# Products for the row maxima over 64 queries of two heads, in an attention and FFN layer on one core

## The chip, the cores and the metric

One core of a Trainium2 chip runs the whole layer in one launch. The metric is the device time of an execution in microseconds; three runs of the kernel before took 827.39, 828.68 and 829.8 us, and their median, 828.68 us, is the time before.

## What is computed

The input `x` is 4 sequences of 512 tokens with 1024 features, in float32. With LN for a layer norm without weights, the layer is:

```python
q = LN(x) @ Wq                        # 32 heads of 32
k, v = split(LN(x) @ Wkv)             # one head of keys and values, shared by the 32
scores = q·k / sqrt(32) + slope[h] * (key_pos - query_pos)     # ALiBi
attn = softmax(scores where key_pos <= query_pos)              # causal
x = x + (attn @ v) @ Wo
w = (six-bit codes unpacked from qweight - zero_point) * scale
x = x + (LN(x) @ w.T + bias)
```

## The kernel before

Products run on TensorE (PE) in `fp32r`; where one such product is not exact enough, both operands are cut in a high and a low part and two or three products are summed (`split` makes the parts: ScalarE copies the high part, VectorE subtracts to get the low one).

**Attention** is done in 32 steps: 4 sequences (`b`) by 8 groups (`g`) of 4 heads (`GH`). The step `i = b * 8 + g` has three parts, and at any time the parts of several steps are under way:

- `queries` computes the 128 rows (4 heads by 32) of q for 512 tokens in 24 products (line 682), splits them into `qh` and `ql`, writes both to the DRAM buffer `q_d` and reads them back three times (high, low, high) into one *query stack* `qs`: rows 0 to 95 are q, 28 more rows (`qr_d`, prepared once for each group) hold the ALiBi slopes and the block-wise causal mask, and two last rows will hold the row maxima. There are three buffers for such stacks. A step so moves 256 KB five times through `q_d`, in runs of 2 KB, and 224 KB from `qr_d`. The moves are issued on SP's queue by the helper at line 420.
- `maxima` needs the largest score of each query and head. It multiplies a block of queries (as weights, 128 columns of the stack) with the keys that it may see (moving). For token tile `t` of 128 queries and head `h` the keys up to `(t + 1) * 128` are taken (line 739): 16 products, four each with 512, 384, 256 and 128 columns. They fill 11 PSUM banks in turn (`S_BANKS`), of which two are there. VectorE adds the triangle `mask` and takes the maximum of each row in one instruction for each product (line 752), into one column of `mx`; the bank is free again after it. One transpose (line 768) turns `mx` into 16 rows of 128, ScalarE and VectorE cut them in two parts `mt`, and two DMAs put them into the last rows of the stack.
- `attention` multiplies the keys (as weights) with the stack: the result `st` (line 820) is the score less the maximum, transposed (keys in partitions). ScalarE takes the exponential into `p`; GpSimd clears what lies above the diagonal, for each of the four key tiles one selection over 4 heads by 128 queries (line 839); `pav` (line 849) multiplies with the values, four heads side by side in the array; GpSimd adds up the `p` of the four tiles (line 861), and `den` (line 878) sums over keys. `a` is copied to DRAM; the denominators are inverted at a sequence's end (`invert`).

After that come 16 token tiles with the output projection `po` (line 1048), the second layer norm and the FFN product `pf` (line 1168). They use nothing of what is changed here.

**Order.** Each operation is written with a wished-for time (`at`), a cost in ns and what it reads and writes. A planner (`Work`) plays the engines forward and backward with these costs and puts out one fixed order for each engine; DMAs count as 450 ns of SP each and then a rate of 280 bytes per ns and 2 us to land, whatever the length of their runs. At run time each engine works its list strictly in that order, and waits where an operand is not there yet; also an operation that could run has to wait behind one that can't. A changed cost or width anywhere can move operations elsewhere.

The lines that say how a step's products are put into banks:

```python
S_BANKS = [((t, h),) for t in (3, 2) for h in range(GH)]
S_BANKS += [tuple((1, h) for h in (2 * i, 2 * i + 1)) for i in range(2)]
S_BANKS += [tuple((0, h) for h in range(GH))]
```

Of the kernel before, what the change touches and what calls it, by code (L numbers as in the profile page):

```python
# [41 lines left out]
P = 128  # L43
NH = 32
HD = 32
GH = 4
S = 512
# [25 lines left out]
def bias_rows():  # L73

    k = np.arange(S)
    block = k // KB
    kr = np.zeros((N_BIAS + 2, S), np.float32)
    kr[0:2] = k - block * KB - KB // 2  # L80
    for r in range(NB):
        kr[2 + r] = kr[2 + NB + r] = block == r
    kr[N_BIAS:] = -1.0
    slopes = alibi_slopes(NH)
    sh, sl = split12(slopes)
    qr = np.zeros((NH, N_BIAS, S), np.float32)
    qr[:, 0] = sh[:, None]
    qr[:, 1] = sl[:, None]
    r = np.arange(NB)
    mid = r[:, None] * KB + KB // 2 - k[None, :]  # L90
    v = slopes[:, None, None] * mid[None]
    v = np.where((r[:, None] > block[None, :])[None], MASKED, v)
    qr[:, 2 : 2 + NB], lo = split12(v)
    qr[:, 2 + NB :] = np.where(v == MASKED, 0.0, lo)
    qr = qr.reshape(NH // GH, GH, N_BIAS, S).transpose(0, 2, 1, 3)
    return kr, np.ascontiguousarray(qr)
# [245 lines left out]
def layer_kernel(  # L342
# [30 lines left out]
    for name, bufs in (  # L373
        ("const", 1), ("w", 2 * NG), ("xc", KC + 2), ("x", 4), ("qs", 3), ("q1", 1), ("p0", 2),
        ("pj", 1), ("stg", 3), ("kv", 2), ("small", 4), ("mt", 2),
    ):
        pool(name, bufs)
# [41 lines left out]
    def move(dst, src):  # L419
        return nc.sync.dma_start(out=dst.bitcast(F32), in_=src.bitcast(F32))  # L420


    qr_d = tc.dram_tile([NG, N_BIAS, GH, S], F32R, name="qr_d")
    at_d = tc.dram_tile([NG, P, B * S], F32, name="at_d")
    q_d = tc.dram_tile([4, 2, P, S], F32R, name="q_d")
# [16 lines left out]
    nc.gpsimd.affine_select(  # L442
        out=mask(),
        in_=mask(),
        pattern=[[-1, S]],
        compare_op=ALU.is_ge,
        fill=MASKED,
        base=S - P,
        channel_multiplier=1,
    )  # L450
# [14 lines left out]
    def prep_rows(at, g):  # L465
        dma(
            at, 229e3, lambda: nc.gpsimd.dma_start(out=qr_d[g], in_=q_rows[g]), [qr_i[g]], [],
            eng="POOL",
        )
# [205 lines left out]
    def queries(at, i):  # L675
        b, g = divmod(i, NG)
        pq = new("ps_q", "q", [P, S], F32, f"pq_{i}")
        hi, lo = wq[g]
        for c in range(KC):
            def three(c=c):  # L680
                for n, (w, s) in enumerate(((hi, 0), (lo, 0), (hi, 1))):
                    nc.tensor.matmul(  # L682
                        pq(), w()[:, c, :], xc[b, c]()[:, s, :],
                        start=(c == 0 and n == 0), stop=(c == KC - 1 and n == 2),
                    )
            h = c // (KC // 2)
            pe(at + 1.3 * c, [S] * 3, three, [pq], [(hi, h), (lo, h), xc[b, c]], more=12.0)
        at += 10.4
        qh = new("q1", "qh", [P, S], F32R, f"qh_{i}")
        ql = new("q1", "ql", [P, S], F32R, f"ql_{i}")  # L690
        split(at, S, qh, ql, pq, qh, ql, pq)

        qs[i] = [(0, GH, new("qs", "qs", [P, GH, S], F32R, f"qs_{i}"))]
        for s, src in enumerate((qh, ql)):
            dma(
                at + 0.6 + 0.7 * s, 262e3,
                lambda s=s, src=src: move(q_d[i % 4, s], src()), [q_i[i % 4][s]], [src],
            )
        for h, n, q in qs[i]:
            dma(  # L700
                at + 1.0, 57e3 * n,
                lambda h=h, n=n, q=q: move(q()[R_BIAS:R_MAX, :, :], qr_d[g, :, h : h + n, :]),
                [(q, "b")], [qr_i[g]],
            )
            for r in range(3):
                dma(
                    at + 3.0 + 0.1 * r, 65e3 * n,
                    lambda r=r, h=h, n=n, q=q: move(
                        q()[ts(r, HD), :, :],
                        q_d[i % 4, r % 2, h * HD : (h + n) * HD].rearrange(  # L710
                            "(h d) q -> d h q", d=HD
                        ),
                    ),
                    [(q, r)], [q_i[i % 4][r % 2]],
                )

    def part(i, h):

        return next((q, h - first) for first, n, q in qs[i] if first <= h < first + n)


    S_BANKS = [((t, h),) for t in (3, 2) for h in range(GH)]
    S_BANKS += [tuple((1, h) for h in (2 * i, 2 * i + 1)) for i in range(2)]
    S_BANKS += [tuple((0, h) for h in range(GH))]
    ROWS = (0, 1, 2, "b")

    def maxima(at, i):
        b = i // NG
        k = kst[b % 2]
        mx = new("small", "mx", [P, GH * NT], F32, f"mx_{i}")  # L730
        for n, bank in enumerate(S_BANKS):
            ps = new("ps_s", "s", [P, S], F32, f"s_{i}_{n}")
            widths = [(t + 1) * P for t, _ in bank]
            places = [sum(widths[:m]) for m in range(len(bank))]

            def products(ps=ps, bank=bank, widths=widths, places=places):
                for (t, h), W, o in zip(bank, widths, places):
                    q, at = part(i, h)
                    nc.tensor.matmul(  # L739
                        ps()[:, o : o + W], q()[0:R_MAX, at, ts(t, P)], k()[0:R_MAX, :W],  # L740
                        start=True, stop=True,
                    )
            pe(
                at + 1.2 * n, widths, products, [ps],
                [(q, r) for q in {part(i, h)[0] for _, h in bank} for r in ROWS] + [k],
                more=sum(45.0 if w == P else 5.0 for w in widths),
            )
            for (t, h), W, o in zip(bank, widths, places):
                junk = new("q1", "junk", [P, S], F32, f"junk_{i}_{t}_{h}")
                dve(  # L750
                    at + 1.2 * n + 0.3, W,
                    lambda ps=ps, junk=junk, t=t, h=h, W=W, o=o: nc.vector.tensor_tensor_reduce(  # L752
                        out=junk()[:, :W],
                        in0=ps()[:, o : o + W],
                        in1=mask()[:, S - W :],
                        scale=1.0,
                        scalar=-3e38,
                        op0=ALU.add,
                        op1=ALU.max,
                        accum_out=mx()[:, h * NT + t : h * NT + t + 1],  # L760
                    ),
                    [(mx, (t, h))], [ps], more=125.0,
                )
        at += 1.2 * len(S_BANKS)
        N = GH * NT
        tr = new("ps_misc", "misc", [P, P], F32, f"trm_{i}")
        pe(
            at, [P], lambda: nc.tensor.transpose(tr()[0:N, :], mx(), ident()), [tr], [mx]
        )
        for s in range(2):  # L770
            m = new("mt", f"mt{s}", [N, P], F32R, f"mt{s}_{i}")
            if s == 0:
                hi = m
                act(at + 0.2, P, lambda: nc.scalar.copy(hi(), tr()[0:N, :]), [hi], [tr])
            else:
                lo = m
                dve(
                    at + 0.4, P,
                    lambda: nc.vector.tensor_tensor(
                        lo(), tr()[0:N, :], hi().bitcast(F32), ALU.subtract  # L780
# [3 lines left out]
            for h, n, q in qs[i]:  # L784
                dma(
                    at + 0.5 + 0.2 * s, 2e3 * n,
                    lambda m=m, s=s, h=h, n=n, q=q: move(
                        q()[R_MAX + s : R_MAX + s + 1, :, :], m()[h * NT : (h + n) * NT, :]
                    ),
                    [(q, f"m{s}")], [m],  # L790
                )
# [6 lines left out]
    def attention(at, i):  # L798
        b, g = divmod(i, NG)
        k = kst[b % 2]  # L800
# [5 lines left out]
        for n, (j, heads) in enumerate(ST_BANKS):  # L806
# [3 lines left out]
            runs = []  # L810
            for first, m, q in qs[i]:
                lo, hi = max(first, heads[0]), min(first + m, heads[-1] + 1)
                if lo < hi:
                    runs.append((
                        q, slice(lo - first, hi - first), slice(lo - heads[0], hi - heads[0])
                    ))

            def products(ps=ps, j=j, runs=runs):
                for q, mine, place in runs:
                    nc.tensor.matmul(  # L820
                        ps()[:, place, :], k()[0:R_ALL, ts(j, P)], q()[0:R_ALL, mine, j * P :],
                        start=True, stop=True,
                    )
            pe(
                at + 1.2 * n, [len(heads) * W / len(runs)] * len(runs), products, [ps],
                [q for q, _, _ in runs] + [k], more=5.0,
            )
# [8 lines left out]
            if done[j] == GH:  # L836
                def select(j=j):
                    d = pr[j]()[:, :, 0:P]
                    nc.gpsimd.affine_select(  # L839
                        out=d, in_=d, pattern=[[0, GH], [1, P]], compare_op=ALU.is_ge,  # L840
# [26 lines left out]
        act(at + 15.4, S, lambda: nc.scalar.copy(a(), pav()), [a], [pav])  # L867
# [16 lines left out]
    def invert(at, b):  # L884
        r = new("stg", "stg", [P, S], F32, f"rec_{b}")
        d = den[b]
        for t in range(NT):
            work.op(
                "DVE", at + 0.1 * t, 840.0,
                lambda t=t: nc.vector.reciprocal(r()[:, ts(t, P)], d()[:, ts(t, P)]),  # L890
# [410 lines left out]
```

## Time and profile before

| | us |
|---|---|
| median of three runs | 828.68 |
| the profiled execution: its own time | 830.86 |
| its span, from the first to the last instruction | 828.9 |
| busy in the span: TensorE | 802.1 |
| busy: VectorE | 572.4 |
| busy: GpSimd | 515.7 |
| busy: ScalarE | 369.4 |
| mean granted TensorE clock | 0.993 |

The profile is of one execution, by the hardware profiler. A line of its groups names the source line, engine, operation, `out<-in` tiles, partitions by elements, the count, then busy time in us and the mean ns of one, then the idle time of the engine just before such instructions and what ended it. `PEld` is the weight loads of TensorE, which run beside its products; `SPq` is SP's queue, which issues DMAs. The time from the first product to the end of the attention is some 540 us of the span; the token tiles follow until 829 us, the first two of them overlapping the last steps.

### The profile page before, as it was taken

What the parts mean: (1) busy time and instruction counts of PE and PEld (TensorE: products, weight loads), DVE (VectorE), ACT (ScalarE), POOL (GpSimd) and SP (SyncE); (2) the same over time, 40 slices, a digit from 0 to 9 for tenths busy, and PEclk for the clock granted to TensorE, in tenths of its full rate; (3) what the DMA queues carried; (4) which work ended last, traced back from release to release, by engine and by line L of the source; (5) the groups of instructions that cost most, each with busy time, mean ns of one, the idle gap of its engine ahead of it and who ended that gap; (6) DMA issues with size and microseconds to landing.
All of it is one profiled execution on the core that took longest, in us unless ns stands there. A gap on an engine that the chain in (4) does not pass through costs nothing.

```text
span 828.9 us, 13434 instructions
## 1 busy us (share of the span) xinstructions
PE 802.1 (97%) x4480; PEld 595.8 (72%) x4480; DVE 572.4 (69%) x1491; ACT 369.4 (45%) x659; POOL 515.7 (62%) x442
## 2 busy tenths in 40 slices
PE   5989999999999999999999999999999999999997
PEld 5766677776566767666766667667888888888885
DVE  7576876478676469866358656645988867678755
ACT  4336664545665354755365564340142323333320
POOL 4337968285968185876388997778556445554323
PEclk9989999999999999999999999999999999999999
DMA  7997662486742397463457774626975675565321
GB/s 221 245 249 214 186 173 63 123 221 216 207 112 82 91 257 227 116 162 113 153 138 220 200 215 141 232 51 165 254 169 137 138 184 127 137 164 131 102 51 51
DMA packets 131796, 133.39 MB, mean 161 GB/s; under 512 B 42964, under 2 KB 93140, under 8 KB 130704
## 3 DMA queue, kind: packets, MB, share of 16 engines
q1 hardware_dynamic: 130912, 129.01, 57.4%
q0 software_dynamic: 816, 3.53, 1.5%
q8 instruction: 35, 0.57, 0.3%
q14 instruction: 33, 0.27, 0.1%
HBM read 85.58 MB, written 39.85 MB: 151 GB/s over the span
## 4 chain that ended last, share of the span: by engine, by line
PE 87%; DMA 4%; DVE 4%; issue 2%; POOL 1%; ACT 1%; SPq 0%; DVEq 0%; ACTq 0%; POOLq 0%
PE po L1048 21%; PE pq L682 18%; PE pf L1168 13%; PE s L739 9%; PE st L820 9%; PE pav L849 8%; PE den L878 3%; PE pkv L616 2%; PE tr L598 2%; DVE junk L752 2%; POOL p L861 1%; DMA q_d<-ql 1%; DMA qs<-q_d 1%; ACT p L830 1%; DMA qs<-qr_d 1%
## 5 line engine op out<-in xcount | busy, mean ns | idle before, releaser
L752 DVE CUSTOM_DVE_ANT_0 junk<-s,mask 128x256 f32<-128x256 f32 (+3 forms) x512 | 250.4, 489 | 123.2 <-PE s L739 92.1
L861 POOL TENSOR_TENSOR p<-p,p 128x1536 f32<-128x1536 f32 (+2 forms) x96 | 230.4, 2400 | 20.2 <-PE pav L849 18.2
L830 ACT ACTIVATE p<-st 128x512 f32<-128x512 f32 (+1 forms) x352 | 184.0, 560 | 115.1 <-PE st L820 111.7
L682 PE MATMUL pq<-xc,wqh 128*128 128x512 f32 x512 | 195.8, 402 | 1.5 <-DVE ql L415 1.4
L1048 PE MATMUL po<-woh,aT 128*128 128x512 f32 x512 | 165.7, 390 | 0.0
L839 POOL TENSOR_SCALAR_AFFINE_SELECT p<-p 128x512 f32<-128x512 f32 x128 | 81.9, 645 | 104.4 <-ACT p L830 103.7
L739 PE MATMUL s<-kst,qs 124*128 124x256 f32 (+3 forms) x512 | 138.4, 339 | 7.0 <-DVE mx L752 3.3
L820 PE MATMUL st<-qs,kst 126*128 126x512 f32 (+1 forms) x352 | 125.6, 395 | 3.1 <-ACT p L830 2.6
L1168 PE MATMUL pf<-wf,xT 128*128 128x512 f32 x512 | 120.8, 390 | 0.7 <-DVE xT L415 0.7
L739 PEld LDWEIGHTS s<-kst,qs 124*128 124x128 f32 x512 | 89.0, 193 | 44.1 <-DVE mx L752 16.3
L682 PEld LDWEIGHTS pq<-xc,wqh 128*128 128x128 f32 x512 | 97.6, 191 | 21.6 <-DVE ql L415 2.1
L1048 PEld LDWEIGHTS po<-woh,aT 128*128 128x128 f32 x512 | 96.2, 188 | 21.4 <-ACT a L867 0.8
L1168 PEld LDWEIGHTS pf<-wf,xT 128*128 128x128 f32 x512 | 95.8, 188 | 21.5 <-DVE xT L415 1.7
L682 PE MATMUL pq<-xc,wql 128*128 128x512 f32 x256 | 101.6, 397 | 0.0
L1048 PE MATMUL po<-wol,aT 128*128 128x512 f32 x256 | 99.7, 390 | 0.0
L820 PEld LDWEIGHTS st<-qs,kst 126*128 126x128 f32 x352 | 65.0, 190 | 24.1 <-ACT p L830 9.7
L849 PE MATMUL pav<-p,kv 128*32 128x512 f32 (+3 forms) x1024 | 79.4, 436 | 0.4 <-POOL p L839 0.4
L849 PEld LDWEIGHTS pav<-p,kv 128*32 128x32 f32 x1024 | 29.9, 109 | 50.7 <-issue 38.0
L1188 POOL TENSOR_TENSOR x<-x,y 128x512 f32<-128x512 f32 x30 | 43.0, 1438 | 26.4 <-DVE y L1179 26.4
L1048 PEld LDWEIGHTS po<-wol,aT 128*128 128x128 f32 x256 | 48.1, 188 | 9.6
L1146 POOL TENSOR_TENSOR x<-x,rows 128x512 f32<-128x512 f32 x32 | 43.9, 1391 | 17.3 <-issue 10.1
L682 PEld LDWEIGHTS pq<-xc,wql 128*128 128x128 f32 x256 | 49.0, 191 | 5.8
(92 smaller groups left out, 850.5 us busy)
## 6 DMA issues: line engine op xcount, KB each, us to landing
qs<-q_d SPq DMA_DIRECT2D x96, 256.0 KB
x<-_attn_hidden_states_dram SPq DMA_DIRECT2D x31, 512.0 KB
q_d<-qh SPq DMA_DIRECT2D x32, 256.0 KB
q_d<-ql SPq DMA_DIRECT2D x32, 256.0 KB
at_d<-a SPq DMA_DIRECT2D x32, 256.0 KB
raw<-at_d SPq DMA_DIRECT2D x16, 512.0 KB
raw<-rden_d SPq DMA_DIRECT2D x64, 128.0 KB
out_dram<-x SPq DMA_DIRECT2D x32, 256.0 KB
```

The lines of the kernel that those rows point to most:

```text
L682: nc.tensor.matmul(pq(), w()[:, c, :], xc[b, c]()[:, s, :], start=(c == 0 and n == 0), stop=(c == KC - 1 and n == 2),)
L739: nc.tensor.matmul(ps()[:, o : o + W], q()[0:R_MAX, at, ts(t, P)], k()[0:R_MAX, :W], start=True, stop=True,)
L752: lambda ps=ps, junk=junk, t=t, h=h, W=W, o=o: nc.vector.tensor_tensor_reduce(out=junk()[:, :W], in0=ps()[:, o : o + W], in1=mask()[:, S - ...
L820: nc.tensor.matmul(ps()[:, place, :], k()[0:R_ALL, ts(j, P)], q()[0:R_ALL, mine, j * P :], start=True, stop=True,)
L830: lambda ps=ps, own=own, j=j: nc.scalar.activation(pr[j]()[:, own, :], ps(), AF.Exp),
L839: nc.gpsimd.affine_select(out=d, in_=d, pattern=[[0, GH], [1, P]], compare_op=ALU.is_ge, fill=0.0, base=0, channel_multiplier=-1,)
L849: nc.tensor.matmul(pav()[ts(h, HD), j * P :], kv[b]()[:, j, HD:], pr[j]()[:, h, :], start=(j == 0), stop=(j == NT - 1), tile_position=(0, ...
L861: nc.gpsimd.tensor_tensor(d, d, pr[j](), ALU.add)
L1048: nc.tensor.matmul(po(), aT[s][1]()[:, c, :], w()[:, ts(n, HALF)], start=(c == 0 and m == 0), stop=(c == KC - 1 and m == 2),)
L1146: nc.gpsimd.tensor_tensor(d, d, rows["bias"][n][1](), ALU.add)
L1168: nc.tensor.matmul(pf(), xT()[:, s, c, :], wf[c]()[:, ts(n, HALF)], start=(c == 0 and s == 0), stop=(c == KC - 1 and s == 1),)
L1188: (nc.vector if last else nc.gpsimd).tensor_tensor(d, d, y(), ALU.add)
```

## The change

The products for the maxima take 64 queries of two heads, side by side as 128 weight columns, in place of 128 queries of one head. A block of 64 queries `e` then needs the keys up to `(e + 1) * 64` alone: 16 products as before, two each with 64, 128, 192, ... 512 columns. The banks are filled as 512, 512, then 448+64, 384+128, 320+192 twice each, then 256+256: nine of them.

For a weight block of two heads and 64 queries to lie at one constant step in the stack, the stack's layout becomes token tile, head, query (before: head, query), and inside each tile of 128 the two halves of 64 are interleaved: query `o * 64 + m` lies at place `2 * m + o`. So the weights are read with a step of two elements. `qh` and `ql` are written in that order, `q_d` holds it in runs of 128 elements (512 B), and `p`, `pav` and `den` have it as well; the copy to `a` and the reciprocal put it back. GpSimd's selection runs over 4 by 64 by 2 in place of 4 by 128. The maxima are two sets of 8 columns, so two transposes turn them, and the copies of `mt` have twice the columns in half the rows; `mt` has one buffer in place of two. `mask` differs from 0 in its last 64 columns alone.

```diff
+QB = 64
...
-        ("pj", 1), ("stg", 3), ("kv", 2), ("small", 4), ("mt", 2),
+        ("pj", 1), ("stg", 3), ("kv", 2), ("small", 4), ("mt", 1),
...
-    q_d = tc.dram_tile([4, 2, P, S], F32R, name="q_d")
+    q_d = tc.dram_tile([4, 2, NT, P, P], F32R, name="q_d")
...
-        split(at, S, qh, ql, pq, qh, ql, pq)
+        def turns(t):
+            return lambda: t().rearrange("p (t m o) -> p t o m", t=NT, m=QB)
+        split(
+            at, S, turns(qh), turns(ql),
+            lambda: pq().rearrange("p (t o m) -> p t o m", t=NT, m=QB), qh, ql, pq,
+        )
+        q = qs[i] = new("qs", "qs", [P, NT, GH, P], F32R, f"qs_{i}")
...
-                lambda s=s, src=src: move(q_d[i % 4, s], src()), [q_i[i % 4][s]], [src],
+                lambda s=s, src=src: move(
+                    q_d[i % 4, s].rearrange("t p q -> p t q"),
+                    src().rearrange("p (t q) -> p t q", t=NT),
+                ),
+                [q_i[i % 4][s]], [src],
...
+                lambda r=r: move(
+                    q()[ts(r, HD)].rearrange("d t h q -> d (t h) q"),
+                    q_d[i % 4, r % 2].rearrange("t (h d) q -> (t h) d q", d=HD).rearrange(
+                        "x d q -> d x q"
                     ),
+                ),
...
-    S_BANKS = [((t, h),) for t in (3, 2) for h in range(GH)]
-    S_BANKS += [tuple((1, h) for h in (2 * i, 2 * i + 1)) for i in range(2)]
-    S_BANKS += [tuple((0, h) for h in range(GH))]
+    NQ = S // QB
+    HP = GH // 2
+    S_BANKS = [((NQ - 1, u),) for u in range(HP)]
+    S_BANKS += [((NQ - 2 - m, u), (m, u)) for m in range(NQ // 2 - 1) for u in range(HP)]
+    S_BANKS += [tuple((NQ // 2 - 1, u) for u in range(HP))]
...
-            widths = [(t + 1) * P for t, _ in bank]
+            widths = [(e + 1) * QB for e, _ in bank]
...
+                    t, o = divmod(e, P // QB)
+                    rows = q()[0:R_MAX, t].rearrange("p h (m o) -> p o (h m)", m=QB)
                     nc.tensor.matmul(
-                        ps()[:, o : o + W], q()[0:R_MAX, at, ts(t, P)], k()[0:R_MAX, :W],
+                        ps()[:, at : at + W], rows[:, o, ts(u, P)], k()[0:R_MAX, :W],
                         start=True, stop=True,
                     )
...
-                more=sum(45.0 if w == P else 5.0 for w in widths),
+                more=sum(max(5.0, 97.0 - w / 2.4) for w in widths),
...
-        pe(
-            at, [P], lambda: nc.tensor.transpose(tr()[0:N, :], mx(), ident()), [tr], [mx]
-        )
+        def turned():
+            for o in range(P // QB):
+                nc.tensor.transpose(tr()[0:N, o, :], mx()[:, o, :], ident())
+        pe(at, [P] * (P // QB), turned, [tr], [mx])
...
-                act(at + 0.2, P, lambda: nc.scalar.copy(hi(), tr()[0:N, :]), [hi], [tr])
+                act(
+                    at + 0.2, 2 * P,
+                    lambda: nc.scalar.copy(hi().rearrange("n m o -> n o m"), tr()[0:N]), [hi], [tr],
+                )
...
-                    d = pr[j]()[:, :, 0:P]
+                    d = pr[j]()[:, :, 0:P].rearrange("p h (m o) -> p h m o", m=QB)
                     nc.gpsimd.affine_select(
-                        out=d, in_=d, pattern=[[0, GH], [1, P]], compare_op=ALU.is_ge,
+                        out=d, in_=d, pattern=[[0, GH], [1, QB], [QB, P // QB]],
+                        compare_op=ALU.is_ge,
                         fill=0.0, base=0, channel_multiplier=-1,
                     )
...
+                a().rearrange("p (t o m) -> p t o m", t=NT, m=QB),
+                pav().rearrange("p (t m o) -> p t o m", t=NT, m=QB),
```

## The prediction

> **What bounds the kernel now.** I read the page from the top: which engine is full, what the chain of waits consists of, then the stage that the change touches, and in it the rows of the products.
>
> ```profile
> PE 802.1 (97%) x4480; PEld 595.8 (72%) x4480; DVE 572.4 (69%) x1491; ACT 369.4 (45%) x659; POOL 515.7 (62%) x442
> PEclk9989999999999999999999999999999999999999
> PE 87%; DMA 4%; DVE 4%; issue 2%; POOL 1%; ACT 1%; SPq 0%; DVEq 0%; ACTq 0%; POOLq 0%
> ```
>
> TensorE (PE) is busy 97% of the span and makes 87% of the chain. So a nanosecond of PE work removed is nearly a nanosecond of time, and work on another engine counts only where PE ends up waiting for it. The sum of busy time by stage shows the same for the attention stage, where the whole change lies (columns: stage, length, busy time of PE, weight loads, VectorE, ScalarE, GpSimd, granted clock, DMA share, GB/s):
>
> ```profile
> 50.00:550.00 500.00, 490.22 (x3084) 340.12 (x3083) 338.42 (x1163) 274.51 (x533) 350.46 (x285) 0.99 0.59 167
> ```
>
> GpSimd has 149.5 us left in these 500 us, 4.7 us for each of the 32 steps; I come back to that. Now the products of the row maxima, by shape, and the one transpose per step (busy, mean ns, then idle time before them and who ended it):
>
> ```profile
> L739 PE MATMUL s<-kst,qs 124*128 124x512 f32 x128 | 51.2, 418 | 3.6 <-issue 1.8 <-DMA qs<-qr_d 0.7 <-DMA qs<-q_d 0.7
> L739 PE MATMUL s<-kst,qs 124*128 124x384 f32 x128 | 44.2, 366 | 2.5 <-DVE mx L752 2.5
> L739 PE MATMUL s<-kst,qs 124*128 124x256 f32 x128 | 26.8, 296 | 0.4 <-DVE mx L752 0.3
> L739 PE MATMUL s<-kst,qs 124*128 124x128 f32 x128 | 19.3, 275 | 0.7 <-DVE mx L752 0.5
> L768 PE MATMUL trm<-ident,mx 128*16 128x128 f32 x32 | 8.7, 273 | 0.0
> ```
>
> The mean durations overlap, so they are no price. The price is the distance from one start to the next, which the timeline gives (start us, length):
>
> ```profile
> 252.60 0.34 PE L739 MATMUL s<-kst,qs 124*128 124x384 f32 x1
> 252.77 0.40 PE L820 MATMUL st<-qs,kst 126*128 126x512 f32 x1
> 253.01 0.41 PE L739 MATMUL s<-kst,qs 124*128 124x256 f32 x2
> 253.25 0.39 PE L820 MATMUL st<-qs,kst 126*128 126x512 f32 x1
> ...
> 255.39 0.56 PE L739 MATMUL s<-kst,qs 124*128 124x128 f32 x4
> 255.88 0.86 PE L849 MATMUL pav<-p,kv 128*32 128x256 f32 x16
> ...
> 258.26 0.63 PE L739 MATMUL s<-kst,qs 124*128 124x512 f32 x2
> 258.73 0.57 PE L820 MATMUL st<-qs,kst 126*128 126x384 f32 x2
> ```
>
> 384 columns take 0.17 us, two of 256 take 0.24, two of 512 take 0.47. But 128 columns take 0.11 to 0.12, no less than 256. Over all steps the median distances between equal neighbours are 236, 177 (384 followed by another kind), 120 and 111 ns. Below 256 columns the weight load sets the pace, not the columns.
>
> **The change, part by part.** Everything is summed against the profiled execution (830.86 us, span 828.9), which is 2.18 us above the median of the runs shown (828.68); the result is moved down by as much.
>
> *Fewer columns.* A step keeps 16 products; their widths go from four each of 128, 256, 384, 512 to two each of 64, 128, ... 512: 5120 columns become 4608. Before: 4 x (236 + 177 + 120 + 111) = 2.58 us. After, with 111 for 64, 128 and 192, and 148, 206 interpolated for 320 and 448: 2 x (333 + 120 + 148 + 177 + 206 + 236) = 2.44 us. Saved 0.136 us a step, on the path: 32 x 0.136 = **-4.4 us**. Half of the columns' saving is lost on the floor of 111 ns.
>
> *A second transpose.* The maxima lie as two sets of 8 columns, so a step issues two transposes. The chain gives one of them 0.11 us; the distance to the next start is 0.07 in the mean. 32 x 0.11 = **+3.5 us** (from 2.2).
>
> *Banks and VectorE.* 11 PSUM banks per step become 9, and the 16 reductions read 512 columns less; from 689 ns at 512 and 291 at 128 columns a column costs 1.04 ns, so 0.53 us a step, 17 us of VectorE in all. VectorE is not the bound; it counts where PE waits for a bank. Over the back-to-back distances the starts of `s` are late by 14.8 us in sum from 50 to 550 us. Two of 11 handovers less: 2/11 x 14.8 = **-2.7 us** (0 to -7.0, PE's whole idle time before L739).
>
> *Shorter runs in the transfers.* `q_d` is written twice and read three times per step, 256 KB each, in runs of 512 B where there were 2 KB. By the trace's packet records a 2 KB packet took 107.8 ns, a 512 B packet 34.6, so four of them 138. For three reads that is 96 packets more per engine than a fourth part would give: 96 x (34.6 - 27.0) = 0.73 us later per stack. Yet neighbouring reads of a stack landed 1.16 us apart, 145 ns per 2 KB and engine, so something else than the packets may set the pace, and the delay may be 0. The far end: loads of 512 KB landed at best after 4.4 us in 512 B runs (`raw`), after 3.3 us in 4 KB runs (`x`), 0.55 us per 256 KB, 1.6 for three. I take 0.5, nearest the packet row, which has the size itself. What does it meet? From semaphore times, the first `s` product of a step starts 0.09 to 5.5 us (median 1.1) after the last of its stack landed; the stack cannot be asked for earlier, because the read waits until the products of three steps before have released the buffer. All else on SP, the next step's stack, `at_d` and the weights, is queued behind it. Summing max(0, delay - slack) over the 32 steps: 0.5 gives 2.9, 0.75 gives 5.4, 1.0 gives 8.6, 1.5 gives 17.6. So **+2.9 us**. [...]
>
> Two lines of the chain in order of time show what such lateness looks like when it does reach PE:
>
> ```profile
> 220.91 5.02 DMA qs<-mt
> 351.44 5.57 DMA qs<-qr_d
> ```
>
> *The way back of the maxima.* The second transpose (0.11), a ScalarE copy of 256 instead of 128 columns (+0.1) and the subtraction (273 to about 424 ns, the row of 256 columns) delay `mt` by 0.35 us, and a fuller queue adds some 0.15. The first `st` product has 0.1 to 9.4 us (median 1.7) after `mt` landed; 0.5 us cost **+0.7 us** (0.2 to 3.5). One buffer instead of two for `mt` waits only for a DMA of a step ago, 15 us back: nothing.
>
> *Start.* The order of the changed kernel issues the next batch's first `x` load after four stacks instead of between two. The second stack landed 0.1 us before its products before, and the clock granted in 50 to 100 us is 0.93, some 3.5 us lost around PE's waits there. I take **-1.0 us** (-4 to +3).
>
> *At nothing:* the interleaved copies of `qh`, `ql`, `a` and the reciprocal keep their element counts; they hide under PE while ScalarE has 45% and VectorE 69%; uncovered, 0.1 us on each of 32 steps would be 3 us. ScalarE's copies that read 16-bit words two apart (1044 ns for 1024, L1099) are no dearer than straight ones (1054, L412).
>
> *Two unknown forms.* The weights of `s` are now read with a step of two elements, and GpSimd's selection of the causal triangle runs over [4, 64, 2] instead of [4, 128]. No weight load of the trace is stepped. Nearest row: the contiguous load, floor 111 ns; far end: half rate. I take the near end. [...] For the selection:
>
> ```profile
> L839 POOL TENSOR_SCALAR_AFFINE_SELECT p<-p 128x512 f32<-128x512 f32 x128 | 81.9, 645 | 104.4 <-ACT p L830 103.7
> L442 POOL TENSOR_SCALAR_AFFINE_SELECT mask<-mask 128x512 f32<-128x512 f32 x1 | 0.6, 612 | 0.1
> ```
>
> Four runs of 128 (median 635) against one of 512 (612): 23 ns for three more runs, or noise of a single row. Near end 0; far end 8 ns for each of 252 more runs, +1.9 us per selection. I take 0 and keep the rest as a rival.
>
> **Sum:** -4.4 + 3.5 - 2.7 + 2.9 + 0.7 - 1.0 = -1.0 us; 830.86 - 1.0 - 2.18 = **827.7 us**. The open ends of the terms, not all at once, make it 820 to 836. About 0.3%, 2.5 us, is what a measurement can tell from no change, so faster means below 826.2, slower above 831.2.
>
> **Rivals.** (1) *GpSimd's selection becomes slow in runs of two.* For: the 23 ns above, and GpSimd's part in every step. Against: GpSimd is 1% of the chain. It decides from 0.64 + 4.7/4 = 1.8 us per selection, where GpSimd fills the step; below that it delays the `pav` products. Doubled, with one length of 0.64 us reaching PE in each step: +20.5, 848 us. At the far end, 4 x 1.9 - 4.7 = 2.9 us a step: 920 us.
> (2) *Stepped weights load at half rate.* 14 of 16 products would take 222 ns: 14 x 222 + 2 x 236 = 3.58 us against 2.44, +36 us, 864 us. It decides as soon as the floor goes from 111 to about 120 ns, where the gain is gone. For: it is untested here. Against: the row that is nearest.
> (3) *Stacks land 1.5 us late instead of 0.5.* The wait for a bank gives way to a wait for the stack: 17.6 - 2.9 = +14.7, 842 us. It decides from about 0.7 us. For: the median slack of 1.1 us and a DMA share of 0.59; against: 1.16 us between landings.
>
> **How the numbers follow.** The sum has 0.66 (0.32 faster, 0.14 same, 0.20 slower, as its range lies around the two bounds); rival 1 has 0.14, 2 has 0.08, 3 has 0.12, all slower. Together 0.32, 0.14, 0.54. The likeliest case alone is 820 to 836; to leave out no more than 2 in 10, the range goes from 819 to 856, past rival 3 and the milder half of rival 1.
>
> **What would show it.** Right: `s` at 111 ns for 64 to 192 columns and 236 at 512, two `trm` per step at 0.11, L839's successor near 640 ns, idle time before `s` from DVE smaller and from `qs` DMAs larger. Wrong: weight loads of `s` longer than 190 ns (rival 2), the selection over 1 us (rival 1), PE idle on `qs<-q_d` beyond 6 us in sum (rival 3). A gain over 8 us would mean that VectorE's banks held PE far more than the 14.8 us that I found.

## The result, and the profile after

The changed kernel took **971.38 us** (median of four runs, 970.49 to 976.85) where the kernel before took 828.88 on the same chip: a ratio of 1.1735 (95% interval 1.1688 to 1.1782), 17% slower. The prediction of 827.7 us, with a range to 856, was wrong by 144 us. The head of the page after, with busy times, granted clock and the chain's shares by engine:

```profile
PE 852.0 (88%) x4512; PEld 621.1 (64%) x4512; DVE 570.0 (59%) x1491; ACT 377.6 (39%) x659; POOL 731.2 (75%) x443
PEclk9998889989998988999997999888899999999999
PE 47%; POOL 40%; issue 4%; DVE 4%; ACT 2%; DMA 2%; SPq 0%; DVEq 0%; POOLq 0%; ACTq 0%
```

GpSimd (POOL) went from 515.7 to 731.2 us busy, and from 1% of the chain to 40%. TensorE has 50 us more busy time, though it multiplies fewer columns: the clock digits fall to 8 and 7 in the attention stage, and products follow each other more slowly where less clock is granted. In this trace the granted clock is either full or half; it is half for 122 us in sum (14 us before). The `pq` products start 427 ns apart there and 232 ns apart at full clock, in the median. TensorE is busy for 108 us of the half-clock time (10 before), so an estimate from these numbers, half of the difference, puts 49 of the 50 us down to the clock. By stage (columns as in the prediction: stage, length, busy times of PE, weight loads, VectorE, ScalarE, GpSimd, clock, DMA share, GB/s):

```profile
50.00:550.00 500.00, 428.43 (x2515) 292.31 (x2514) 279.26 (x977) 234.17 (x437) 437.89 (x229) 0.92 0.52 131
550.00:700.00 150.00, 124.99 (x675) 83.71 (x674) 65.56 (x191) 52.12 (x99) 138.62 (x70) 0.87 0.48 127
```

The attention's last selection now ends at 688 us instead of 562, and up to there GpSimd is the fuller engine. The groups name the instruction (mean ns of one after the comma), and behind the last bar who made TensorE wait:

```profile
L847 POOL TENSOR_SCALAR_AFFINE_SELECT p<-p 128x512 f32<-128x512 f32 x128 | 298.0, 2341 | 46.1 <-ACT p L838 45.8
...
L894 PE MATMUL den<-p,onesel 128*32 128x512 f32 x256 | 38.7, 680 | 18.6 <-POOL p L870 18.6
...
L858 PE MATMUL pav<-p,kv 128*32 128x128 f32 x256 | 15.1, 313 | 31.1 <-POOL p L847 31.1
```

The selection of the causal triangle took 645 ns and takes 2341. TensorE now stands before `pav`, the product that needs the cleared `p`, and before `den`, which needs the sum of the four `p`. The chain in order of time shows how this reaches the end (start us, length, what):

```profile
301.52 3.51 POOL p L870
305.03 2.28 POOL p L847
307.30 2.35 POOL p L870
309.66 2.28 POOL p L847
311.93 1.24 POOL p L870
313.17 2.06 POOL p L847
...
323.95 3.85 PE pkv L620 x16
```

Selections (L847) and additions (L870) follow each other on GpSimd with hardly a gap (0.16 us at most); TensorE appears only after 22 us of it.

### The profile page after: what moved, and what is told of

Read it like the earlier page. It is cut to its first block, busy times and chain, and to the rows that moved or that the text cites. A ratio compares the mean times of both kernels' runs of the same rounds, so it can differ in the third digit from the quotient of the medians.

```text
span 970.0 us, 13447 instructions
## 1 busy us (share of the span) xinstructions
PE 852.0 (88%) x4512; PEld 621.1 (64%) x4512; DVE 570.0 (59%) x1491; ACT 377.6 (39%) x659; POOL 731.2 (75%) x443
## 4 chain that ended last, share of the span: by engine, by line
PE 47%; POOL 40%; issue 4%; DVE 4%; ACT 2%; DMA 2%; SPq 0%; DVEq 0%; POOLq 0%; ACTq 0%
POOL p L847 22%; PE po L1067 17%; POOL p L870 14%; PE pf L1187 11%; PE pq L686 8%; PE st L830 3%; PE s L749 3%; PE pav L858 2%; POOL wol L493 1%; ACT p L838 1%; DMA wo_st<-in_L_attn_Wo_dram 1%; DVE junk L763 1%; PE pkv L620 1%; PE den L894 1%; PE tr L602 1%
## 5 line engine op out<-in xcount | busy, mean ns | idle before, releaser
L763 DVE CUSTOM_DVE_ANT_0 junk<-s,mask 128x448 f32<-128x448 f32 (+7 forms) x512 | 233.6, 456 | 208.0 <-PE s L749 182.3
L847 POOL TENSOR_SCALAR_AFFINE_SELECT p<-p 128x512 f32<-128x512 f32 x128 | 298.0, 2341 | 46.1 <-ACT p L838 45.8
L870 POOL TENSOR_TENSOR p<-p,p 128x1536 f32<-128x1536 f32 (+2 forms) x96 | 229.6, 2392 | 6.2 <-PE pav L858 4.9
L686 PE MATMUL pq<-xc,wqh 128*128 128x512 f32 x512 | 207.4, 422 | 2.3 <-DVE ql L420 1.6
L830 PE MATMUL st<-qs,kst 126*128 126x512 f32 (+1 forms) x352 | 139.3, 432 | 21.3 <-ACT p L838 21.1
L858 PE MATMUL pav<-p,kv 128*32 128x512 f32 (+3 forms) x1024 | 96.1, 474 | 46.5 <-POOL p L847 46.2
L749 PE MATMUL s<-kst,qs 124*128 124x448 f32 (+7 forms) x512 | 126.5, 333 | 5.8 <-DVE mx L763 4.2
L749 PEld LDWEIGHTS s<-kst,qs 124*128 124x128 f32 x512 | 102.5, 214 | 39.4 <-issue 14.9
L686 PEld LDWEIGHTS pq<-xc,wqh 128*128 128x128 f32 x512 | 102.4, 200 | 21.6 <-DVE ql L420 1.4
L830 PEld LDWEIGHTS st<-qs,kst 126*128 126x128 f32 x352 | 69.7, 206 | 49.7 <-ACT p L838 33.3
L542 POOL TENSOR_SCALAR rstd_f<-mv_f 128x1 f32<-128x1 f32 x16 | 5.9, 372 | 76.6 <-DVE mv_f L537 76.5
```

Of the source, the lines that this page charges most:

```text
L686: nc.tensor.matmul(pq(), w()[:, c, :], xc[b, c]()[:, s, :], start=(c == 0 and n == 0), stop=(c == KC - 1 and n == 2),)
L749: nc.tensor.matmul(ps()[:, at : at + W], rows[:, o, ts(u, P)], k()[0:R_MAX, :W], start=True, stop=True,)
L763: nc.vector.tensor_tensor_reduce(out=junk()[:, :W], in0=ps()[:, place : place + W], in1=mask()[:, S - W :], scale=1.0, scalar=-3e38, op0=A ...
L830: nc.tensor.matmul(ps().rearrange("p h (t q) -> p h t q", q=P), k()[0:R_ALL, ts(j, P)], q()[0:R_ALL, j:, own].rearrange("p t h q -> p h t q"),
L847: nc.gpsimd.affine_select(out=d, in_=d, pattern=[[0, GH], [1, QB], [QB, P // QB]], compare_op=ALU.is_ge, fill=0.0, base=0, channel_multipl ...
L858: nc.tensor.matmul(pav()[ts(h, HD), j * P :], kv[b]()[:, j, HD:], pr[j]()[:, h, :], start=(j == 0), stop=(j == NT - 1), tile_position=(0, ...
```

## The experiments

Theory A: the runs of two in the selection make GpSimd the bound, and that is the loss. The rivals: the stacks come late because of the 512-B runs (theory B); the stepped weights load slowly (theory C in the texts of e1, e2 and e4); and, from e5 on, an order of the operations that happens to be worse (rival C in the later texts). The kernel before was run again beside each group of experiments, with medians of 828.4 to 828.9 us. The edits are shown shortened.

**e1: the selection without runs of two.** The changed kernel, with each selection as two, one for each half, each over four runs of 64.

```diff
-  out=d, in_=d, pattern=[[0, GH], [1, QB], [QB, P // QB]], base=0
+  for o in range(2):  # d = d[:, :, :, o], a step of two in memory
+    out=d, in_=d, pattern=[[0, GH], [1, QB]], base=o * QB
```

> The changed kernel, but each selection of the causal triangle on GpSimd is made by two instructions of 4 by 64 elements (step two, runs of 64) in place of one over 4 by 64 by 2. Theory A, that the runs of two made the selection slow and GpSimd the bound: a selection of 256 elements takes about 0.40 us, GpSimd's busy time falls from 731 to some 540 us, the granted clock returns to 0.98 or more, and the time to 815 to 835 us (827.7 by the sum of the prediction; about 820 if the pairs of products that now fill a bank cost 240 ns as in the trace after). Theory B, that the stacks in runs of 512 B come late: above 840 us, with PE idle on the stack's reads. Theory C, that weights read with a step load at half rate: 850 us or more, weight loads of s longer than 190 ns at full clock.

841.13 us, ratio 1.0144 (1.0118 to 1.0169). All but 12 us of the loss is gone. The time is 6 us above theory A's range, though, and inside theory B's, so what makes these 12 us is open here. The two selections together take 886 ns, where 0.8 us was expected:

```profile
L848 POOL TENSOR_SCALAR_AFFINE_SELECT p<-p 128x256 f32<-128x256 f32 x256 | 103.9, 443 | 81.0 <-ACT p L838 81.0
```

**e2: the runs of two alone.** The kernel before, in which the same elements of the selection, in the same places, are described as runs of two. Nothing else is changed.

```diff
-  pattern=[[0, GH], [1, P]]
+  pattern=[[0, GH], [2, P // 2], [1, 2]]
```

> The kernel before, with one edit: the same selection is written over 4 by 64 by 2 elements, so the same elements and the same result in runs of two. Theory A: 2.3 us per selection and 950 to 990 us, as much as the whole change. Theories B and C: no other part of the change is in it, so at most 5 us over the kernel before.

963.98 us, ratio 1.1639 (1.1605 to 1.1673): +135 us from this edit alone. The traces have the instructions of every engine in the same order as before.

```profile
PE 851.7 (88%) x4480; PEld 616.9 (64%) x4480; DVE 589.5 (61%) x1491; ACT 371.8 (39%) x659; POOL 728.3 (76%) x442
...
L839 POOL TENSOR_SCALAR_AFFINE_SELECT p<-p 128x512 f32<-128x512 f32 x128 | 297.4, 2338 | 54.0 <-ACT p L830 54.0
```

With e1 this settles the main question from both sides: taken out of the changed kernel the runs of two free 130 us, put into the old one they cost 135.

**e3: the price of a run.** Twelve selections more at the start of the kernel before, on the still empty mask: 512 elements in runs of 512, 256, 128, 64, 32, 16, 8, 4 and 2, then the changed kernel's own form, then 256 elements of it in four runs of 64, with and without a step of two.

> The kernel before, with twelve selections more at its start, on a tile of zeros of 128 by 512, in runs of 512, 256, 128, 64, 32, 16, 8, 4 and 2, then 4 by 64 by 2, then 256 elements as 4 by 64 with a step of two, then the same with a step of one. It times the selection by itself. Theory A, a price per run: from 612 ns for one run and 2323 for 256 runs of two, 6.7 ns per run, so 0.61, 0.62, 0.63, 0.66, 0.71, 0.82, 1.04, 1.46 and 2.32 us, then 2.32, and 0.40 for each of the last two. A rival, that only a third dimension or only a step makes it slow: all runs in two dimensions near 0.64, and 2.3 for 4 by 64 by 2 alone.

The kernel's one run took 840.9 us; its time is not of interest. The timeline, with the runs of 512, 128, 8 and 2 and the form of the changed kernel:

```profile
1.94 0.61 POOL L443 TENSOR_SCALAR_AFFINE_SELECT mask<-mask 128x512 f32<-128x512 f32 x1
...
3.31 0.63 POOL L443 TENSOR_SCALAR_AFFINE_SELECT mask<-mask 128x512 f32<-128x512 f32 x1
...
6.43 1.08 POOL L443 TENSOR_SCALAR_AFFINE_SELECT mask<-mask 128x512 f32<-128x512 f32 x1
...
9.21 2.31 POOL L443 TENSOR_SCALAR_AFFINE_SELECT mask<-mask 128x512 f32<-128x512 f32 x1
11.59 2.32 POOL L443 TENSOR_SCALAR_AFFINE_SELECT mask<-mask 128x512 f32<-128x512 f32 x1
```

In ns, for 1, 2, 4, 8, 16, 32, 64, 128 and 256 runs: 612, 619, 634, 657, 717, 837, 1083, 1564, 2307. Counted from the single run, each further run costs 6.4 to 7.5 ns; the values lie near one straight line (the last doubling is cheaper, 5.8 ns a run). The rival in the text, that only a third dimension or a step is slow, falls: these nine have neither. All nine read the same contiguous 2 KB of each partition, so it is the shape of the pattern that costs, not the place in memory. A step of two in memory is nearly free: 437 ns against 414 for 256 elements.

**e4: the stack in 512-B runs.** The kernel before with the stack and `q_d` laid out by token tile, in natural order; the products for the maxima, the selection and the single transpose are those of before (`qr_d`, the columns of `mx` and the operand of `st` follow the layout).

```diff
-  q_d = tc.dram_tile([4, 2, P, S], F32R)
+  q_d = tc.dram_tile([4, 2, NT, P, P], F32R)
-  qs: [P, GH, S]
+  qs: [P, NT, GH, P]
```

> The kernel before with the changed kernel's stack layout alone: token tile before head, written and read through the DRAM buffer in runs of 512 B, with no interleaving, no change of products, selections or transposes. Theory A: the term of the prediction, +2.9 us (0 to +8.6), so 829 to 837 us. Theory B: +15 us or more, 843 us up. Theory C: as A.

838.39 us, ratio 1.013 (1.0093 to 1.0166), between the ranges of theory A and theory B. The idle time before the 512-wide products, 3.6 us before, is now mostly the stack's:

```profile
L736 PE MATMUL s<-kst,qs 124*128 124x512 f32 x128 | 51.6, 424 | 8.5 <-DMA qs<-qr_d 4.0 <-DMA qs<-q_d 2.0 <-issue 1.0
```

This speaks for theory B as the cause of the remaining 12 us of e1. But the version also had DMA sizes in the planner that differ by 1%, and so another order than before; e7 was made for that.

**e5: an order that knows.** The changed kernel, with the selection planned at 2350 ns instead of 650.

> The changed kernel, with one number of the planner changed: a selection in runs of two is planned with 2350 ns instead of 650. The instructions are the same, their order is another. Theory A (GpSimd's own work is the bound: some 11 us a step before and 4 x 1.7 = 6.8 us more now, 17.9 us a step, 32 x 17.9 = 573 us after about 70 us of start, 280 us of token tiles behind it, part of them overlapping): the time stays high, 930 to 970 us. Rival (the loss comes from an order that plans with a wrong cost): most of it goes, below 880 us.

940.11 us (930.47 to 941.41), ratio 1.1323. The order gives back 31 us and the rest stays. In the stage of the attention GpSimd is busy 92.5% of the time (462.69 of 500 us):

```profile
50.00:550.00 500.00, 453.89 (x2699) 300.40 (x2698) 315.92 (x1032) 239.22 (x458) 462.69 (x230) 0.97 0.54 136
```

The chain of this run reads otherwise than that of the changed kernel:

```profile
PE 64%; DVE 12%; DMA 8%; issue 6%; POOL 5%; ACT 3%; SPq 2%; DVEq 0%; ACTq 0%; POOLq 0%
```

TensorE waits for a selection only 2.8 us before `pav` (46.2 in the changed kernel), and the loss comes through several engines. From 62 to 655 us GpSimd is busy 550 us, which is 57 us more than the whole such stretch took before (62 to 555 us). An estimate from this is that about half of the remaining 111 us is GpSimd's work alone; the other half was not taken apart.

**e7: another order, and nothing else.** The kernel before with e4's DMA sizes in the planner.

> The kernel before, with the planner's DMA sizes of the query stack rounded up by about 1% (262e3 for 260e3, 229e3 for 228e3, 8e3 for 8e3); the instructions are the same, only their planned order moves. It is the control of the kernel before with the 512-B stack, which had these sizes too and took 838.4 us. Theory B (the shorter runs make the stacks late and cost nearly 10 us): this stays at 827 to 831 us. Rival C (any other fixed order costs several us): 833 to 840 us.

832.03 us (828.49 to 834.93), ratio 1.0039 (1.0023 to 1.0055), between the ranges of theory B and rival C. A change of 1% in planned sizes alone costs 3.7 us. The instructions are the same, so this is order alone. The traces of e4 and e7 have the same instructions in the same order on every engine, so e7 is the control that e4 needs: of e4's 10 us the order makes 3.7 and the layout, in that order, 6.4 (838.39 to 832.03, with intervals of the ratios that do not meet). Of these, 3.1 us are idle time of TensorE on the stack's DMAs before the 512-wide products (6.0 in e4, 2.9 here). 14 of the 32 steps of this kernel also start their products less than 0.75 us after their stack landed (11 in the kernel before, 19 in e4).

```profile
L739 PE MATMUL s<-kst,qs 124*128 124x512 f32 x128 | 51.5, 423 | 4.3 <-DMA qs<-qr_d 1.8 <-DVE mx L752 1.2 <-DMA qs<-q_d 1.1
```

**e9: natural `p`.** The changed kernel, but ScalarE's exponential writes `p` in natural order; the selection, `pav`, `den`, `a` and the reciprocal are those of before. The planned costs are those of the changed kernel.

```diff
-  nc.scalar.activation(pr[j]()[:, own, :], ps(), AF.Exp)
+  nc.scalar.activation(
+      pr[j]()[:, own, :].rearrange("p h (t o m) -> p (h t) o m", o=2, m=QB),
+      ps().rearrange("p h (t m o) -> p (h t) o m", o=2, m=QB), AF.Exp)
...
-  pattern=[[0, GH], [1, QB], [QB, P // QB]]
+  pattern=[[0, GH], [1, P]]
```

> The changed kernel, but ScalarE's exponential puts the halves back in order when it writes p, so that the selection has its four runs of 128 again, and pav, den, a and the reciprocal are as in the kernel before; the interleaved stack, the 64-query products, the two transposes and the 512-B runs stay, and the planned order is that of the changed kernel. Theory A (runs of two are the loss): selections at 645 ns again, time 828 to 840. If ScalarE's exponential is dearer when it reads two elements apart, its mean of some 490 ns rises and the time with it (840 to 860). Theory B (the rest of the loss of the version with two selections, 841.1 us, is the stacks' lateness): 836 to 841, no better than that version. If that rest was GpSimd's 0.24 us more per tile: 828 to 833.

840.49 us (834.40 to 844.31), ratio 1.0139 (1.0107 to 1.017). The selection is back at 648 ns, and the time is that of e1, inside theory B's 836 to 841: GpSimd's 0.24 us more per selection in e1 cost nothing that can be told from this. The exponential that puts the halves back costs nothing either (597 ns for 512 columns, 598 before). So the length of the selection does not explain the remaining 12 us.

```profile
L848 POOL TENSOR_SCALAR_AFFINE_SELECT p<-p 128x512 f32<-128x512 f32 x128 | 82.3, 648 | 92.5 <-ACT p L838 92.0
```

**e10 and e11: planned costs, and writes of 2 KB.** e10 is e9 with two planned costs corrected; e11 is e10 with `q_d` in rows of 512 queries, so that its writes run over 2 KB and only its reads over 512 B.

```diff
-  more=sum(max(5.0, 97.0 - w / 2.4) for w in widths)   # products of the maxima
+  more=5.0 * len(widths)
-  pe(at, [P] * (P // QB), turned, [tr], [mx])
+  pe(at, [P] * (P // QB), turned, [tr], [mx], more=80.0)
```

> The version before this one in the list, with two planned costs corrected by what the runs showed: short products of the maxima at their columns (no floor of 111 ns when they alternate with long ones) and 80 ns more for the pair of transposes. Only the order moves. Rival C (order): differs from it by several us, down to 828. Theory B (stacks): within 3 us of it.

> The version with the natural p and the two corrected costs (834.7 us), but q_d keeps rows of 512 queries, so that it is written in runs of 2 KB and only read in runs of 512 B; the planned order is the same. Theory B (the stacks' lateness is what is left, and the shorter runs make it): two of five transfers of q_d land some 0.3 us earlier, half of the steps wait for their stack, so about 16 x 0.3 = 5 us less, 829 to 832 us. Rival (the runs' length does not matter, the order does): 833 to 836.

834.65 us (829.95 to 838.96), ratio 1.0065 (1.0039 to 1.0092), and 833.73 us (830.65 to 837.28), ratio 1.0056 (1.0036 to 1.0077). The new order brought 5.8 us, the longer writes nothing that can be told from no change: theory B's 5 us did not come.

**e12: reads planned longer.** As e11, with a read of the stack planned at 340e3 bytes instead of 262e3. No instruction is another.

> As the one before, and the planner is told 340e3 bytes instead of 262e3 for a read of the stack, 1.3 times as much, as the packet records of 512 B and 2 KB have it (138 to 108 ns), so that it plans products of the maxima later after the reads. Only the order moves. Theory B: 825 to 830 us, PE idle before the 512-wide products below 3 us. Rival: within 2 us of the one before, since a fixed order cannot move the reads, which wait for a free buffer.

828.14 us (826.74 to 830.75, 12 runs), ratio 0.9991 (0.9979 to 1.0002): the time of the kernel before, with an interval that just reaches it. Theory B's forecast came true here, the rival's did not: TensorE hardly waits for the stacks' reads before its 512-wide products any more (0.6 us):

```profile
L744 PE MATMUL s<-kst,qs 124*128 124x512 f32 x64 | 24.3, 420 | 1.5 <-DMA qs<-mt 0.7 <-DMA qs<-q_d 0.6
```

**e13 and e14: transposes apart.** As e12, with another order of the banks and the two transposes as operations of their own; in e14 the reads are planned with 300e3 bytes.

```diff
-  def turned(): (both transposes) ... pe(at, [P] * 2, turned, [tr], [mx])
+  for o, when in ((1, at - 3.0), (0, at)):
+      pe(when, [P], transpose of half o, [(tr, o)], [columns of half o])
```

> The version before this (828.1 us) with the banks in the order 512, 512, 320+192 twice, 256+256, 448+64 twice, 384+128 twice, so that the eight columns of the odd blocks are complete halfway, and the two transposes as operations of their own, so that each can stand between longer products. In that version two neighbouring transposes cost 112 ns from start to start and the second 26. If a transpose between other products costs 30 ns as the one of the kernel before does (median 29), 32 x 0.08 = 2.6 us go: 825 to 827 us. Rival (the order that comes out of it is worth more than that): anything from 824 to 833.

> The same instructions as in the run before, with the planned size of a read of the stack at 300e3 instead of 340e3, so another order. If the order's share is small: within 1.5 us of the run before. Rival C (order): up to 6 us away.

835.66 us (ratio 1.0089, 1.0067 to 1.0112) and 840.01 us (1.0147, 1.0122 to 1.0171), both worse than e12; e13 lies above both of its ranges, and the order alone moves e14 4.4 us from it. In e13 a transpose does fall to a median of 29 ns between other products, but 2.6 us of idle time on VectorE's maxima, and 4.9 us before the 512-wide products, stand against the gain:

```profile
L779 PE MATMUL trm<-ident,mx 128*8 128x128 f32 x64 | 16.1, 273 | 2.9 <-DVE mx L759 2.6 <-DVE xc L420 0.2
```

The way from the changed kernel down to e12, by medians:

| version | us | step |
|---|---|---|
| after | 971.4 | |
| e9: selection in runs of 128 | 840.5 | -130.9 |
| e10: two planned costs corrected | 834.7 | -5.8 |
| e11: writes in runs of 2 KB | 833.7 | -0.9 (not clear of noise) |
| e12: reads planned longer | 828.1 | -5.6 |
| before | 828.9 | |

No version beats the kernel before by more than a measurement can tell.

## Why the prediction was wrong, point by point

**The step that failed: "For the selection ... I take 0 and keep the rest as a rival."** The two rows that the prediction showed (635 ns for four runs, 612 for one) held the price: 8 ns for each further run. It was called "noise of a single row", and the near end was taken. e3 measures 7.3 ns between the same two shapes and 6.6 in the mean up to 256 runs, so the far end, +1.9 us, was 0.2 us too high and otherwise right. The prediction's own sign for this, a selection over 1 us, came. The mechanism of rival 1 was the one that happened, its turning point (1.8 us per selection, where GpSimd fills the step) lies below the 2.34 measured, and it had 0.14 of the chance and most of its price outside the range. The argument against it, "GpSimd is 1% of the chain", said that GpSimd was not the bound before; it said nothing of an engine whose most frequent instruction becomes 3.6 times as long.

**The size of rival 1.** It said 920 us, and it came out at 971 (940 with the order of e5). The added work is 128 x 1.70 = 217 us of GpSimd. The far end of 920 filled all of GpSimd's free time with work. From 62 to 690 us in the changed kernel GpSimd was busy 561.5 of 628 us; the 66 us in which it was not are more than the whole difference to 920. The fixed order, planned at 650 ns, makes 31 us of the difference (e5). In the same stretch the granted clock was 0.91 (1.00 from 62 to 555 us before), so part of the difference is slower products (`pq` 427 ns apart at half clock, 232 at full).

**Fewer columns: -4.4 predicted, some -14 by the distances measured.** The mis-sized term is "111 for 64, 128 and 192". That floor stood in the trace where products of 128 columns follow each other. In the changed kernel each short product follows a long one, and the timeline shows a pair of 384 and 128 columns take 0.23 us (from its start to that of the next line), no more than the 0.23 of one product with 512:

```profile
303.15 0.40 PE L749 MATMUL s<-kst,qs 124*128 124x384 f32 x2
303.38 0.61 PE L602 MATMUL tr<-ident,x 128*128 128x128 f32 x4
...
304.30 0.40 PE L686 MATMUL pq<-xc,wql 128*128 128x512 f32 x1
304.53 0.39 PE L686 MATMUL pq<-xc,wqh 128*128 128x512 f32 x1
```

The median distances from one start to the next in e12 are 29, 60, 90, 121, 149, 178, 208 and 236 ns for 64 to 512 columns. Twice their sum is 2.14 us a step, against the predicted 2.44 and the 2.58 of before: 32 x 0.44 = 14 us saved. Two loads at the old floor of 111 ns fit beside a pair of 237 ns. In the trace after, the load of the short product's weights runs beside the long product: at full clock it starts a median 3 ns after the long one, and 201 ns before its own product with 448 and 64 columns, 173 with 384 and 128, 144 with 320 and 192. In the trace before, between products of 128 columns, it starts 51 ns after the product ahead and 60 ns before its own; the loads are 111 ns apart there like the products, and no two loads of `s` in a row start less than 108 ns apart. I read these distances as the load setting the pace there, and not where it has a long product beside it; no run took it apart.

**A second transpose: +3.5 predicted.** Start-to-start distances after `trm` summed to 2.2 us before, 7.0 in e1 and 8.0 in e12, waits among them: +4.8 to +5.8. Of a neighbouring pair one costs 112 ns and the other 27 (medians in e12).

**Stepped weights at full rate:** right. The weight loads of `s` last 193 ns in the mean before and 198 in e12, and a pair of 448 and 64 columns takes 237 ns, where two loads at half rate, an estimate from the 111 ns of before, would need 2 x 222. Rival 2 is refuted. Its sign, weight loads of `s` longer than 190 ns, was set too low: the contiguous loads of before already took 193. ScalarE, which reads the scores in PSUM two elements apart in e9, took 597 ns against 598.

**512-B runs: +2.9 predicted, 6.4 in the one order in which it was measured (e4 against e7).** The term was too small by half, but inside the 0 to 8.6 that e4's text gave it. The delay itself was well sized: the stack's reads landed a median 4.17 us after their issue before, 4.65 in the changed kernel and 4.48 in e4; in e12 4.87. What it costs depends on the order: 6 us of idle time before the 512-wide products came from the stack's DMAs in e4, 2.9 in e7, which has the old runs of 2 KB, and 0.6 in e12, which has runs of 512 B. In the changed kernel itself it was mostly hidden (1.5 us of such idle time), since TensorE was late for other reasons. The 0.9 us of the longer writes (e11) cannot be told from nothing. Rival 3 is near e1 and e9 in size (842 us), but no trace has its delay of 1.5 us: in the versions with 512-B reads they land a median 0.3 to 0.7 us later than before. In e12 they land 0.7 us later and the kernel loses nothing, because its order leaves them room: 11 of 32 steps start their products less than 0.75 us after their stack, as many as before, where e9 has 16. What the 512-B reads cost in e12's order stays open, because reads of 2 KB were not run in it.

**Banks: -2.7 predicted.** Idle time before `s` that VectorE ended was 3.3 us before and 1.6 in e12: -1.7, inside the range of the term. The way back of the maxima and the start were not taken apart.

**The sum without the selection** would, with the columns right, have been near -10 us. e12 got 0.8. Its profiled execution lies 4.0 us below that of before (826.86 to 830.86): the products of the maxima gave 16.6 us, the transposes took 5.8 and the distances after the `st` products 4.3, of which 1.9 are idle time before `st` (3.1 before, 5.0 in e12, 4.6 of it on `p` from ScalarE); the rest of those 4.3 is unexplained.

## What to carry to other kernels

Before a layout is interleaved, go through every instruction that walks over it and count the innermost runs of its pattern: a selection over the same contiguous elements in 256 runs instead of 4 was 3.6 times as long (2338 ns against 645 in e2), and 128 of them took an engine from 1% of the chain to 41%. Two rows that differ by three runs are a price, not noise, as soon as the change multiplies the runs by 64; take the slope or give the far end the larger part of the chance. And where a fixed order is planned from costs, moving a cost by 1% moved this kernel by 3.7 us (e7), so an edit that promises 5 us can only be judged with the order's own spread beside it.

## What the runs showed of the hardware that was not expected

- GpSimd's selection costs 6.4 to 7.5 ns for each innermost run of its pattern beyond the first, on top of 612 ns for 512 elements of float32 in each of 128 partitions (e3), while a step of two elements in memory adds only 6% (437 against 414 ns for 256 elements). The 3.6-fold time (2338 ns against 645) came in e2 with no step at all.
- A short product that follows a long one (448 or 384 columns) started its successor after 29 ns for 64 and 60 ns for 128 columns in e12, where 128-column products in a row took 111 ns each in the kernel before.
- With the longer selection TensorE's granted clock fell too: e2 changes nothing but GpSimd's selection, and the mean granted clock of the profiled execution falls from 0.993 to 0.947, the time at half clock rises from 14 to 104 us, and TensorE's busy time by 50 us for the same products.
